# Local attention after a recurrence: V as the stationary operand, and the softmax divided ahead of the transposes

## The chip, the cores and the metric

The kernel runs on one core of a Trainium2 chip. The metric is the device time of one execution in microseconds: the median of three runs was 3732.54 us (3727.72 to 3736.64). The profile is that of one more execution, which took 3730.44 us.

In this document PE is TensorE (matrix products), PEld its loads of stationary operands, DVE is VectorE, ACT is ScalarE, POOL is GpSimd and SP is SyncE, which issues most of the transfers.

## The reference

The input x has 8 sequences of 512 tokens with 128 features. Everything is in float32.

1. x is normalised and goes through a recurrence over the 512 tokens, `h = tanh(h @ A.T + xb_t)`, `y = h @ C.T`; the result is normalised and added to x.
2. Then come six layers. Each has local attention with 16 heads of 64 features and windows of 32 tokens, followed by a feed-forward layer with a GELU gate. In both, half of the features are first shifted by one token.

The part of the attention that matters here is:

```python
q = l2norm(q) * qs ; k = l2norm(k) * ksc        # then rotary tables
sim = einsum('bhwie,bhwje->bhwij', bq, bk2) * 8.0   # 32 queries, 64 keys
sim = where(mask, -max, sim)
attn = softmax(sim, -1)
out = einsum('bhwij,bhwje->bhwie', attn, bv2)
x = out @ Wo + x
```

A window of 32 queries looks at its own 32 keys and at the 32 before them.

## The kernel before, in words

The work of the attention is cut into **groups**. In layers 1 to 5 a group is one sequence and eight heads (class `Group`); in layer 0 it is a stretch of 128 tokens of four sequences and eight heads (class `ChunkGroup`), so that the attention can start while the recurrence still runs. There are 96 groups, 16 to a layer. The eight heads are four pairs (`GP = 4`); `par` names the head of a pair.

A group takes four **slots** (`slot(n, t)`, t = 0 to 3), one for each 128 queries. In slot t of group n the program issues work of four groups:

- the attention of group n itself (`cur`): `scores` (q times k, 32 products of 64 rows by 32 columns, added to a mask that ScalarE has written into the same PSUM tile `sc`), `less_max` (the maximum and the difference), `exps`, and `mask` for the next slot;
- the end of the attention of the slot before (`last`): `turn` transposes the exponentials and copies them to `eT`, `average` multiplies them with V, `divide` divides;
- preparation of group n + 1 (`one`): `sums`, `solve`, `spread` and `finish` normalise q and k (ten Newton steps on VectorE, L450 to L456, and four scalings, L565), `values` makes V, `between` moves halves of it by transfers;
- preparation of group n + 2 (`two`): `unit_a` and `unit_b` project q and k. Their PSUM tiles rawa and rawb are read by ScalarE (L530, L542, L544), VectorE (L516) and, through `bs`, POOL (L548, L549).

In slot 1 the group before (`old`) is multiplied with Wo (`project`, four steps) and added to the residual (`add`).

In the kernel before, `average` takes the exponentials as the stationary operand and V as the moving one, for each head and window. V has a 65th column of ones (`VW = DH + 1`), so the same product gives the sum of the exponentials:

```python
av[blk * QB : (blk + 1) * QB, i, :VW],
self.eT[rows, i, blk * QB : (blk + 1) * QB],   # stationary: 64 rows, 32 queries
self.v[rows, BT * t + blk, i, :],              # moving: 65 columns
```

The result has queries on the partitions. `divide` takes the reciprocal of the 65th column and multiplies, for each `par`; `turn_back` transposes the result one slot later and ScalarE copies it to `aoT`, which `project` reads.

The program is written under a manual schedule: each engine runs its instructions in the order in which the Python code issues them. `mixed` is that order for the groups that run beside the recurrence (the first nine), `dense` for all later ones. The recurrence is driven by `rec.tick(us)`: after enough issued work it puts one more step (a product with A, L281, and a tanh, L289) into the queues; where the attention needs tokens that the recurrence has not reached, `alone` runs steps with filler products. A `Feed` puts the feed-forward layer of four sequences beside a group: shifting and centring in slots 0 and 1, the products of L890 to L923 in slot 2. This is so for eleven groups with four sequences and for one near the end with two.

PSUM tiles come from pools: "acc" has two buffers, taken in turn by `turn`, `turn_back` and the two tiles of `average` (and by the output of the feed-forward layer); "mm" has four (three while the recurrence runs), for projections, values, sums and spreads. `sc` is a single tile.

Of the kernel before, what the change touches and what calls it, by code (L numbers as in the profile page):

```python
# [15 lines left out]
P = 128  # L16
# [11 lines left out]
GP = 4  # L28
# [7 lines left out]
VW = DH + 1  # L36
# [12 lines left out]
def mk_seq_preln_kernel(  # L49
# [44 lines left out]
    for i in range(2):  # L94
        vb = const.tile([P, NBLK, GP, VW], F32, name=f"vbuf{i}")
        nc.gpsimd.memset(vb, 0.0)
        nc.gpsimd.memset(vb[:, :, :, DH:], 1.0)
        vbufs.append(vb)
# [53 lines left out]
    with tc.tile_pool(name="qk", bufs=2) as qkp, tc.tile_pool(  # L152
# [323 lines left out]
        class Group:  # L476
# [174 lines left out]

            def turn(self, t):
                nm = f"{self.nm}_{t}"
                tp = accp.tile([P, GP, P], F32, tag="acc", name=f"tp_{nm}")
                for i in range(GP):
                    nc.tensor.transpose(  # L656
                        tp[:, i, :], self.e[:, i].rearrange("p a k -> p (a k)"), ident
                    )
                rec.tick(0.5)
                self.eT = ep.tile([P, GP, P], F32, tag="eT", name=f"eT_{nm}")  # L660
                nc.scalar.copy(self.eT, tp)  # L661

            def average(self, t):
                self.avs = [
                    accp.tile(
                        [P, GP, P], F32, tag="acc", name=f"av_{self.nm}_{t}_{par}"
                    )
                    for par in range(2)
                ]
                for i in range(GP):  # L670
                    for blk in range(BT):
                        for par, av in enumerate(self.avs):
                            rows = slice(par * KB, (par + 1) * KB)
                            nc.tensor.matmul(  # L674
                                av[blk * QB : (blk + 1) * QB, i, :VW],
                                self.eT[rows, i, blk * QB : (blk + 1) * QB],
                                self.v[rows, BT * t + blk, i, :],
                                start=True,
                                stop=True,
                                skip_group_check=True,  # L680
                            )
                rec.tick(0.8)

            def divide(self, t):
                nm = f"{self.nm}_{t}"
                self.ao[t] = ep.tile(
                    [P, GP, 2, DH], F32, tag="ao", name=f"ao_{nm}", bufs=1
                )
                for par, av in enumerate(self.avs):
                    rc = small.tile([P, GP], F32, tag="rc", name=f"rc_{nm}_{par}")  # L690
                    nc.vector.reciprocal(rc, av[:, :, DH])  # L691
                    nc.vector.tensor_mul(  # L692
                        self.ao[t][:, :, par, :],
                        av[:, :, :DH],
                        rc.unsqueeze(2).to_broadcast([P, GP, DH]),
                    )

            def turn_back(self, t):
                if t == 0:
                    self.aoT = aop.tile([P, GP, S], F32, tag="ao", name=f"aoT_{self.nm}")  # L700
                at = accp.tile([P, GP, P], F32, tag="acc", name=f"at_{self.nm}_{t}")
                for i in range(GP):
                    nc.tensor.transpose(  # L703
                        at[:, i, :], self.ao[t][:, i].rearrange("p a d -> p (a d)"), ident
                    )
                rec.tick(0.5)
                nc.scalar.copy(self.aoT[:, :, t * P : (t + 1) * P], at)  # L707
# [262 lines left out]
        def mixed(n, t, cur, one, two, old, last, lt, back, bt):  # L970
# [10 lines left out]
            if old and t == 1:  # L981
                fill[3] = [lambda: old.project(wo)]
# [22 lines left out]
            if back:  # L1005
                back.turn_back(bt)
# [10 lines left out]
            if one and t == 1:  # L1017
                one.finish(1)
            if last:
                last.average(lt)  # L1020
# [4 lines left out]
            if last:  # L1025
                last.divide(lt)
# [24 lines left out]
        def dense(t, cur, one, two, old, last, lt, back, bt, feed):  # L1051

            def softmax():
                if cur:
                    cur.less_max(t)
                    cur.exps()
                    if t + 1 < NT:
                        cur.mask(t + 1)
                    elif one:
                        one.mask(0)  # L1060

            if last:
                last.turn(lt)
            if back:
                back.turn_back(bt)
            u = 2 * t - 4
            if two and t >= 2 and not (feed and t == 2):
                two.unit_a(u)
            if cur:
                cur.scores(t)  # L1070
            if t == 0:
                softmax()
                if one:
                    one.sums()
                    one.values(0)
                    one.inv.solve()
                if feed:
                    feed.centre(range(0, feed.nb // 2))
                elif one:
                    one.values(1)  # L1080
                    one.between(0)
                if feed:
                    feed.centre(range(feed.nb // 2, feed.nb))
                elif one:
                    one.values(2)
                if last:
                    if not cur:
                        fill(2)
                    last.average(lt)
                    last.divide(lt)  # L1090
                if one:
                    one.spread(range(4))
                    one.finish(0)
            if t == 1:
                softmax()
                if old and not cur:
                    fill(1)
                if old:
                    old.project(wo, (0, 1))
                if one:  # L1100
                    one.finish(1)
                if last:
                    last.average(lt)
                    last.divide(lt)
                if old:
                    old.project(wo, (2, 3))
                    old.add()
                if one:
                    one.finish(2)
                    one.finish(3)  # L1110
# [8 lines left out]
            if t >= 2:  # L1119
                if two and not (feed and t == 2):  # L1120
                    two.unit_b(u)
                softmax()
                if last:
                    if not two:
                        fill(1)
                    last.average(lt)
                    if feed and t == 2:
                        feed.scale()
                    last.divide(lt)
# [14 lines left out]
        def slot(n, t, feed=None):  # L1144
# [10 lines left out]
            back, bt = (cur, t - 2) if t > 1 else (old, NT - 2 + t)  # L1155
            if n < NREC:
                mixed(n, t, cur, one, two, old, last, lt, back, bt)
            else:
                dense(t, cur, one, two, old, last, lt, back, bt, feed)
# [141 lines left out]
def _layout(i):  # L1301
# [17 lines left out]
    w = np.concatenate([qk, v], 2)  # L1319
    b1 = col(i["L0_ffn_b1"])  # L1320
    for base in (0, DI):
# [11 lines left out]
        "w_o": np.asarray(i["L0_ffn_Wo"]),  # L1333
# [24 lines left out]
```

## Time and profile before

| what | value |
|---|---|
| median of three runs | 3732.54 us (3727.72 to 3736.64) |
| the profiled execution | 3730.44 us; its span, first to last instruction, 3728.5 us |
| mean granted TensorE clock | 0.979 |
| a plain group of layer 3, from scores to scores (2005.18 to 2034.17) | 28.99 us |
| 0 to 177 us: the recurrence alone | TensorE busy 150.8 us, VectorE 75.3 |
| 177 to 626 us: groups beside the recurrence | TensorE busy 385.9 us, VectorE 253.0 |
| 912.8 to 3646 us: layers 1 to 5 | TensorE busy 2665.0 us of 2733.2, VectorE 2011.6, ScalarE 1517.5 |

How to read it: busy time is the time in which an engine had an instruction in work. The chain of work goes back from the last instruction, at each step to what released it, so its pieces are the work that set the end. In a line of a group of instructions, the numbers after the count are the busy time in us, the mean of one in ns, the idle time of the engine ahead of them, and what ended that. A matmul in float32 is two instructions.

### The profile page before, as it was taken

The numbers are of one execution on the slowest core, as the hardware profiler recorded it, in microseconds if no ns is written. First come the engines' busy times: TensorE is split into PE (matmuls) and PEld (weight loads), VectorE is DVE, ScalarE is ACT, GpSimd is POOL, SyncE is SP. The second block draws the span as 40 slices with busy tenths as digits, with TensorE's granted clock in tenths as the row PEclk, the third lists the DMA queues.
The fourth block names the chain that finished last, engine by engine and source line by source line (L and its number), as shares of the span: only waits on it lengthen the run. The fifth ranks groups of instructions, "written<-read, shape, count | busy, mean of one in ns | idle before, by whom it ended". The sixth has DMA issues, their size and how long they took to land.

```text
span 3728.5 us, 158927 instructions
## 1 busy us (share of the span) xinstructions
PE 3540.4 (95%) x70178; PEld 2134.8 (57%) x70180; DVE 2587.2 (69%) x5211; ACT 1929.4 (52%) x3864; POOL 1826.7 (49%) x780
## 2 busy tenths in 40 slices
PE   8888987999999999999999999999999999999998
PEld 4566654555566555556566566565566565566564
DVE  3455565767677677677677677677677677677674
ACT  2344443545556455455466455466456455455452
POOL 1442332636466366366366366366366466466460
PEclk9888988999999999999999999999999999999999
DMA  3233433554355355345355345355355355355352
GB/s 129 52 90 84 101 76 84 124 122 103 87 115 116 73 117 129 80 110 119 71 117 133 80 106 123 68 115 138 74 117 116 69 126 126 74 115 118 70 117 70
DMA packets 355866, 378.20 MB, mean 101 GB/s; under 512 B 93550, under 2 KB 254572, under 8 KB 355052
## 3 DMA queue, kind: packets, MB, share of 16 engines
q1 hardware_dynamic: 354172, 365.78, 42.8%
q8 instruction: 554, 9.08, 1.0%
q10 hardware_dynamic: 1008, 2.27, 0.2%
q14 instruction: 132, 1.08, 0.1%
HBM read 34.56 MB, written 14.20 MB: 13 GB/s over the span
## 4 chain that ended last, share of the span: by engine, by line
PE 80%; DVE 11%; ACT 4%; issue 3%; SPq 1%; DMA 1%; DVEq 0%; ACTq 0%
PE yo L713 8%; PE rawb L538 8%; PE rawa L526 8%; PE sc L627 8%; PE av L674 5%; PE tp L656 5%; PE nsq L430 4%; PE at L703 4%; PE xb L281 3%; PE yf L916 3%; PE fa L890 3%; PE fg L894 3%; PE vps L587 3%; PE bc L465 3%; PE warm L361 2%
## 5 line engine op out<-in xcount | busy, mean ns | idle before, releaser
L548 POOL TENSOR_TENSOR u<-rope_sb,bs 128x1024 f32<-128x1024 f32 x320 | 766.4, 2395 | 1225.2 <-ACT bs L544 1090.0
L549 POOL TENSOR_TENSOR t<-t,u 128x1024 f32<-128x1024 f32 x320 | 756.8, 2365 | 25.1
L516 DVE SCALAR_TENSOR_TENSOR t<-rawa,par_sb,rope_sb 128x1024 f32<-128x1024 f32 x320 | 410.3, 1282 | 215.2 <-ACT sq L530 199.6
L650 ACT ACTIVATE e<-e 128x512 f32<-128x512 f32 x320 | 201.7, 630 | 371.4 <-DVE e L643 236.1
L565 DVE TENSOR_TENSOR t<-t,bc 128x1024 f32<-128x1024 f32 x320 | 381.7, 1213 | 15.0 <-PE bc L465 9.8
L661 ACT COPY eT<-tp 128x512 f32<-128x512 f32 x320 | 190.2, 594 | 353.0 <-PE tp L656 352.5
L674 PEld LDWEIGHTS av<-vbuf,eT 64*32 64x32 f32 x20480 | 227.3, 106 | 214.3 <-issue 138.1
L526 PE MATMUL rawa<-xbuf,wqk 128*128 128x512 f32 x640 | 342.8, 617 | 0.0
L538 PE MATMUL rawb<-xbuf,wqk 128*128 128x512 f32 x640 | 342.4, 617 | 0.0
L587 PE MATMUL vps<-wv,xbuf 128*64 128x256 f32 x2560 | 316.4, 387 | 8.4 <-DVE xf L864 8.4
L713 PE MATMUL yo<-aoT,wo 128*128 128x512 f32 x640 | 317.0, 618 | 0.3 <-ACT aoT L707 0.3
L627 PEld LDWEIGHTS sc<-kbuf,qT 64*32 64x32 f32 x20480 | 228.0, 105 | 144.7 <-ACT sq L542 57.6
L692 DVE TENSOR_TENSOR ao<-av,rc 128x256 f32<-128x256 f32 x640 | 271.5, 424 | 22.0
L674 PE MATMUL av<-vbuf,eT 64*32 64x65 f32 x20480 | 281.8, 225 | 3.7 <-issue 3.7
L627 PE MATMUL sc<-kbuf,qT 64*32 64x64 f32 x20480 | 282.8, 225 | 1.9 <-issue 1.8
L640 DVE TENSOR_REDUCE mx<-sc 128x8 f32<-128x512 f32 x320 | 219.3, 685 | 89.1 <-PE sc L627 89.0
L281 PEld LDWEIGHTS xb<-hT,s1w 128*128 128x128 f32 x1022 | 168.3, 197 | 173.8 <-ACT hT L289 118.7
L596 ACT COPY vbuf<-vps 128x512 f32<-128x512 f32 x320 | 188.1, 588 | 138.1 <-PE vps L587 134.7
L542 ACT ACTIVATE sq<-rawb 128x512 f32<-128x512 f32 x320 | 189.8, 593 | 129.7 <-PE rawb L538 129.1
L587 PEld LDWEIGHTS vps<-wv,xbuf 128*64 128x64 f32 x2560 | 168.4, 136 | 152.1 <-DVE rc L691 48.5
L289 ACT ACTIVATE hT<-xb 128x8 f32<-128x8 f32 x512 | 91.5, 179 | 293.8 <-PE xb L281 278.5
L908 DVE SCALAR_TENSOR_TENSOR pr<-fa,b,gl 128x512 f32<-128x512 f32 x144 | 106.8, 748 | 183.0 <-ACT gl L902 178.9
(282 smaller groups left out, 6392.1 us busy)
## 6 DMA issues: line engine op xcount, KB each, us to landing
qT<-t SPq DMA_DIRECT2D x640, 128.0 KB
kbuf<-t SPq DMA_DIRECT2D x640, 128.0 KB
vbuf<-vbuf SPq DMA_DIRECT2D x544, 130.0 KB
vbuf<-vbuf SPq DMA_DIRECT2D x160, 97.5 KB
wqk<-in_w_qkv SPq DMA_DIRECT2D x12, 512.0 KB
xbuf<-xT SPq DMA_DIRECT2D x48, 128.0 KB
xf<-xT SPq DMA_DIRECT2D x24, 256.0 KB
xf<-xT SPq DMA_DIRECT2D x24, 255.5 KB
```

The lines of the kernel that those rows point to most:

```text
L281: nc.tensor.matmul(self.xb[:, k, :], abc[:, 0, :], self.hT[:, (t - 1) % P, :], start=False, stop=True, skip_group_check=True,)
L516: nc.vector.scalar_tensor_tensor(t, self.twice(raw), scale, self.rope(isk, 1), ALU.mult, ALU.mult)
L526: nc.tensor.matmul(raw, self.wqk[:, c, 0], self.xs[:, WINDOW:], start=True, stop=True)
L538: nc.tensor.matmul(raw, self.wqk[:, c, 1], self.xs[:, WINDOW:], start=True, stop=True)
L548: nc.gpsimd.tensor_mul(self.wide(u), self.rope(isk, 0), self.twice(bs))
L549: nc.gpsimd.tensor_add(self.ts[c], self.ts[c], u)
L565: nc.vector.tensor_mul(t, t, self.bcs[c].unsqueeze(1).to_broadcast([P, 2, S]))
L587: nc.tensor.matmul(ps[par * KB : (par + 1) * KB, j], self.xs[:, k0 : k0 + KB], self.wv[:, par * GP * DH : (par + 1) * GP * DH], start=True ...
L627: nc.tensor.matmul(self.sc[blk * QB : (blk + 1) * QB, par, i, :], self.qT[rows, i, q0 : q0 + QB], kT[rows, i, :], start=False, stop=True, ...
L674: nc.tensor.matmul(av[blk * QB : (blk + 1) * QB, i, :VW], self.eT[rows, i, blk * QB : (blk + 1) * QB], self.v[rows, BT * t + blk, i, :], s ...
L692: nc.vector.tensor_mul(self.ao[t][:, :, par, :], av[:, :, :DH], rc.unsqueeze(2).to_broadcast([P, GP, DH]),)
L713: nc.tensor.matmul(self.yp, wo[:, self.g * GP + c, :], self.aoT[:, c, :], start=(c == 0), stop=(c == GP - 1),)
```

## The change

`average` now takes V as the stationary operand (64 keys by 64 features) and the transposed exponentials as the moving one (32 queries). The result has features on the partitions, two heads to a tile: pairs i and i + 1 give the lower and upper half. ScalarE copies it to `aoT` straight away, in two copies of 256 columns, so `turn_back` and its call are gone. V has no column of ones any more. `divide` now works on the exponentials of the slot itself: a sum over the keys, a reciprocal that is written to a tile of "acc", and a product into a new tile `p`, which `turn` transposes in the next slot. The rows of Wo are ordered for the new pairing ahead of the launch. The order in `mixed` and `dense` changes with it: `scores` comes ahead of `turn`, in slots 2 and 3 `unit_a` follows `turn`, the average comes before `unit_b`, and in slot 1 the four steps of `project` come together ahead of the average.

```diff
-VW = DH + 1
+VW = DH
...
-        nc.gpsimd.memset(vb[:, :, :, DH:], 1.0)
...
+            def divide(self, t):
+                nm = f"{self.nm}_{t}"
+                sm = small.tile([P, GP, 2], F32, tag="rc", name=f"sm_{nm}")
+                nc.vector.reduce_sum(sm, self.e, AX.X)
+                rcp = accp.tile([P, GP, P], F32, tag="acc", name=f"rc_{nm}")
+                rc = rcp[:, :, :2]
+                nc.vector.reciprocal(rc, sm)
+                self.p = ep.tile([P, GP, 2, KB], F32, tag="p", name=f"p_{nm}")
+                nc.vector.tensor_mul(
+                    self.p, self.e, rc.unsqueeze(3).to_broadcast([P, GP, 2, KB])
+                )
+
             def turn(self, t):
...
-                        tp[:, i, :], self.e[:, i].rearrange("p a k -> p (a k)"), ident
+                        tp[:, i, :], self.p[:, i].rearrange("p a k -> p (a k)"), ident
...
             def average(self, t):
...
+                order = [
+                    (j + half, blk)
+                    for j in range(0, GP, 2)
+                    for blk in range(BT)
+                    for half in range(2)
+                ]
+                for i, blk in order:
+                    half = slice(i % 2 * DH, (i % 2 + 1) * DH)
+                    cols = slice(blk * QB, (blk + 1) * QB)
+                    for par, av in enumerate(avs):
+                        rows = slice(par * KB, (par + 1) * KB)
+                        nc.tensor.matmul(
+                            av[half, i // 2, cols],
+                            self.v[rows, BT * t + blk, i, :],
+                            self.eT[rows, i, cols],
...
+                for par, av in enumerate(avs):
+                    nc.scalar.copy(
+                        self.aoT[:, 2 * par : 2 * par + 2, t * P : (t + 1) * P],
+                        av[:, :2],
+                    )
...
-            def divide(self, t):
-                nm = f"{self.nm}_{t}"
-                self.ao[t] = ep.tile(
-                    [P, GP, 2, DH], F32, tag="ao", name=f"ao_{nm}", bufs=1
-                )
-                for par, av in enumerate(self.avs):
-                    rc = small.tile([P, GP], F32, tag="rc", name=f"rc_{nm}_{par}")
-                    nc.vector.reciprocal(rc, av[:, :, DH])
-                    nc.vector.tensor_mul(
-                        self.ao[t][:, :, par, :],
-                        av[:, :, :DH],
-                        rc.unsqueeze(2).to_broadcast([P, GP, DH]),
-                    )
-
-            def turn_back(self, t):
-                if t == 0:
-                    self.aoT = aop.tile([P, GP, S], F32, tag="ao", name=f"aoT_{self.nm}")
-                at = accp.tile([P, GP, P], F32, tag="acc", name=f"at_{self.nm}_{t}")
-                for i in range(GP):
-                    nc.tensor.transpose(
-                        at[:, i, :], self.ao[t][:, i].rearrange("p a d -> p (a d)"), ident
-                    )
-                rec.tick(0.5)
-                nc.scalar.copy(self.aoT[:, :, t * P : (t + 1) * P], at)
...
-        def dense(t, cur, one, two, old, last, lt, back, bt, feed):
+        def dense(t, cur, one, two, old, last, lt, feed):
+            u = 2 * t - 4
+            plain = two and t >= 2 and not (feed and t == 2)
+            if cur:
+                cur.scores(t)
             if last:
                 last.turn(lt)
-            if back:
-                back.turn_back(bt)
...
+            if cur:
+                cur.less_max(t)
+            if plain:
                 two.unit_a(u)
             if cur:
-                cur.scores(t)
+                cur.exps()
+                if t + 1 < NT:
+                    cur.mask(t + 1)
...
             if t == 1:
...
                 if old:
-                    old.project(wo, (0, 1))
+                    old.project(wo)
                 if one:
                     one.finish(1)
                 if last:
                     last.average(lt)
-                    last.divide(lt)
+                if cur:
+                    cur.divide(t)
+                if one:
+                    one.finish(2)
                 if old:
-                    old.project(wo, (2, 3))
                     old.add()
                 if one:
-                    one.finish(2)
                     one.finish(3)
...
             if t >= 2:
-                if two and not (feed and t == 2):
-                    two.unit_b(u)
-                softmax()
                 if last:
...
                     last.average(lt)
-                    if feed and t == 2:
-                        feed.scale()
-                    last.divide(lt)
+                if plain:
+                    two.unit_b(u)
+                if feed and t == 2:
+                    feed.scale()
+                if cur:
+                    cur.divide(t)
```

## The prediction

> **What bounds the kernel now.** I read the page's engine shares first, then its chain of work that ended last.
>
> ```profile
> span 3728.5 us, 158927 instructions
> ...
> PE 3540.4 (95%) x70178; PEld 2134.8 (57%) x70180; DVE 2587.2 (69%) x5211; ACT 1929.4 (52%) x3864; POOL 1826.7 (49%) x780
> ...
> PE 80%; DVE 11%; ACT 4%; issue 3%; SPq 1%; DMA 1%; DVEq 0%; ACTq 0%
> ```
>
> TensorE is nearly always busy and carries the chain, but shares say nothing of one stage. So I took one plain group of layer 3 (four slots, no feed-forward beside it), 2005.2 to 2034.2 us, and read the chain through it; this is its start.
>
> ```profile
> 2005.25 0.79 PE sc L627 x53
> 2006.04 1.05 PE rawb L538 x2
> 2007.10 0.79 PE av L674 x53
> 2007.89 1.05 PE rawa L526 x2
> 2008.94 0.87 PE rawb L538 x2
> 2009.82 0.64 PE tp L656 x4
> 2010.46 0.44 PE at L703 x4
> 2010.89 0.86 PE rawa L526 x2
> 2011.76 0.79 PE sc L627 x53
> ```
>
> All 31 pieces of that chain are TensorE's, so a plain group is TensorE's own work. A projection costs 0.86 us, and 1.05 right after a tiled operation (sc, av): leaving the tiles costs 0.19. Next, busy time in the four slots of the group (score to score: slots 2, 3, 0, 1).
>
> ```profile
> core 0: us, PE busy (x) PEld busy (x) DVE busy (x) ACT busy (x) POOL busy (x), PEclk, DMA share, GB/s
> 2005.18:2011.68 6.50, 6.50 (x145) 3.48 (x144) 5.72 (x10) 4.33 (x8) 3.22 (x2) 1.00 0.63 139
> 2011.68:2018.27 6.59, 6.59 (x151) 3.71 (x150) 4.58 (x9) 5.03 (x11) 6.51 (x4) 1.00 0.20 45
> 2018.27:2026.96 8.69, 8.69 (x257) 6.94 (x256) 7.08 (x19) 5.03 (x10) 8.53 (x4) 1.00 0.54 121
> 2026.96:2034.17 7.21, 7.21 (x147) 3.96 (x146) 5.68 (x10) 3.00 (x6) 0.69 (x1) 1.00 0.80 183
> ```
>
> The reader is to see how little room the others have: VectorE 23.1 us of 29.0, ScalarE 17.4, most of it in slots 2, 3 and 0. The granted clock is 1.00. Last, the groups that the change touches.
>
> ```profile
> L692 DVE TENSOR_TENSOR ao<-av,rc 128x256 f32<-128x256 f32 x640 | 271.5, 424 | 22.0
> L674 PE MATMUL av<-vbuf,eT 64*32 64x65 f32 x20480 | 281.8, 225 | 3.7 <-issue 3.7
> L643 DVE TENSOR_TENSOR e<-sc,mx 128x512 f32<-128x512 f32 x320 | 221.1, 691 | 11.0
> L640 DVE TENSOR_REDUCE mx<-sc 128x8 f32<-128x512 f32 x320 | 219.3, 685 | 89.1 <-PE sc L627 89.0
> L707 ACT COPY aoT<-at 128x512 f32<-128x512 f32 x320 | 193.8, 605 | 3.0 <-PE at L703 2.8
> L703 PE MATMUL at<-ident,ao 128*128 128x128 f32 x1280 | 192.4, 273 | 2.2 <-DVE ao L692 2.2
> L691 DVE RECIPROCAL rc<-av 128x4 f32<-128x4 f32 x640 | 111.4, 174 | 44.5 <-PE av L674 34.1
> ```
>
> **The change part by part**, per slot (384 in all: 96 groups of four).
>
> TensorE loses the four transposes back: 0.44 on the chain. The average keeps 32 products in two passes, 64 loads and 64 matmuls, but on four tiles of 64x64 instead of eight of 64x32: 16 passes a tile instead of 8. Loads become 64 columns, moved operands 32. No row has this form. Loads took 106 ns at 32 columns and 136 at 64 (the values, L587): 0.94 ns a column, 60 ns for 64. A 512-column matmul starts 0.43 us after the one before: 0.84 ns a column, 27 for 32. In the transposes 128 columns load and 128 move every 0.11 us, so the load hides behind the previous move, and a pass costs the longer of the two. Now that is the load: 16 x 60 = 0.96, with 0.15 of start 1.1 us instead of 0.79. I take 1.1, as the transposes are the nearest row for loads as long as the moves. Lower end 0.79 (same instruction count at the same pace), upper end 1.55: load and move one after the other, 16 x 87 = 1.39, and the start. In slot 1 the projection is no longer cut by the average, which saves two leavings and adds one for the transposes: 0.3. Per group TensorE's work changes by -4 x 0.44 + 4 x 0.31 - 0.3 = -0.8 us (-2.1 at 0.79, +1.0 at 1.55).
>
> Two rules speak on the average. The Trainium skill (TensorEngine Tiling (Array Packing), Instruction Overhead) says that a free dimension of 1 takes as long as 60, so a small dimension should not be made smaller: moving 32 instead of 65 would gain nothing, a pass would keep its 0.1 us (0.79 over 8 passes of a tile), and 16 passes would give 1.6; the total would then be near rival B's 4035. The same skill's TensorE: Matmul & The Clock Gate ("Wait — 56ns, not 53.3ns?") says that matmuls never start less than about 25 ns apart: 64 x 25 = 1.6, before as after, which would take 4 x 0.31 off a group's bill. Here 64 start within 0.64 us (the 0.86 that one average's matmuls span, less the 0.22 of the last), 10 ns apart: the second rule does not hold in this trace; whether the first does, no row shows.
>
> VectorE loses two reciprocals and two products, 2 x (0.17 + 0.42) = 1.20, and gains a sum (0.685, as the maximum L640), a reciprocal (0.17) and a product over 512 (0.69, as L643): 1.55, so 1.4 more per group. The ends of the new rows are near: 0.6 and 0.7. ScalarE loses a copy of 512 columns (0.605) and gains two of 256. With 0.18 for 8 columns (L289) and 0.60 for 512, 256 cost 0.385: 0.77, 0.17 more; ends 0.30 and 0.60 each.
>
> The order is what costs. Before, the transposes took the exponentials themselves; division came after the average and fed only the transposes back, a slot later. Now sum, reciprocal and product stand between the exponentials and the transposes. The reciprocal goes to a tile of the pool "acc", which has two buffers, taken in turn by tp, av, av, rc. So the reciprocal waits until ScalarE has copied the first av, and that average stands late in TensorE's order. Behind the waiting reciprocal VectorE's queue holds the product, two of the scalings L565 (1.21 each), the residual addition and the next maximum.
>
> I laid the four slots out by hand, each engine in program order with the rows' durations, 0.20 us from a matmul's end to its reader and 0.04 to 0.05 between other engines. The old order comes to 28.96 us a group (measured 28.99). The new one, from the scores of slot 1:
> - TensorE: scores 0.0, transposes, four projection steps to 4.97, average 5.07 to 6.08, scores of slot 2 to 6.79.
> - VectorE: sum to 4.63, then idle for 2.1 us; ScalarE's first copy ends at 6.67, product 6.92 to 7.61. TensorE's transposes start at 7.66: wait 0.8.
> - VectorE is now late: scaling, addition, scaling to 10.56, the maximum of slot 2 10.50 to 11.19, difference 11.92, exponentials 12.60, mask 13.18. The scores of slot 3 wait 0.3.
> - Product of slot 2 14.03 to 14.72: transposes wait 0.75.
> - ScalarE, held behind these exponentials, still owes five readings of slot 2's projections (L542, L544, L530, L542, L544: 3.2 us) before it copies the transposes at 17.70: the average of slot 3 waits 1.5.
>
> Another 0.2 goes before the projection; then the values give the queues time to catch up. Layout against layout, TensorE's work with its changes of tiling goes from 28.4 to 27.4 (-1.0, near the -0.8 above) and its waits from 0.5 to 3.5; a group takes 30.9: **+1.9 us**. It is +1.2 with an average at 0.79, +2.9 at 1.43, +3.3 at 1.55 (a longer average eats some of the waits).
>
> 75 groups are plain: 75 x 1.9 = +143 us. Twelve have a feed-forward beside them: its products hide lateness in slot 2, but slot 1 is VectorE's (two scalings and a Newton solve behind the same reciprocal), ends +0.5 and +3, taken as +2: +24. In the nine first groups the recurrence fills in: each slot loses a transpose and the step after it (0.65 us, as these follow each other in the trace), some 33 slots, -21; the thirty steps that go, by the new program's order, are run alone later at 0.655, +20; longer averages +11, one wait fewer or more unknown (-10 to +20): about +5.
>
> POOL's products (18.95 us a group) start some 2.4 us later, since their input is read after the average; 10 us of idle time cover that, and the key transfers on SP's queue, issued behind the L565 scalings, follow 2 us later into 13 us of margin. SP issues the same transfers (130 KB become 128), and POOL two memsets fewer at the start. These cost nothing while a group stays over 21 us.
>
> Sum: 3730.4 (the profiled run's time, 2 us under the median) + 143 + 24 + 5 = 3902; **3900**. Own range of this case 3830 to 4000 (averages of 0.79 and 1.43, with feed-forward and recurrence at their ends).
>
> **Rivals.** (A) Faster: the product is ready when TensorE comes to transpose, and -0.8 x 87 groups makes 3665. For it: VectorE and ScalarE sum to 25 and 20 of 29 us. Against: their work is bunched in slots 1 to 3. It decides where TensorE's waits grow by less than 0.8 us a group. (B) Load and move do not overlap on a tile: 1.55, 75 x 3.3 + 36 + 20 = +304, 4035. For it: no row shows a long load behind a short move more than twice in a row (the recurrence's pairs, 128 columns loaded and 8 moved, span 0.39 us, so start 0.13 apart). Against: the transposes. (C) VectorE's operations overlap by more than 0.05 us, or the copies take 0.3: half the waits go, 75 x 0.5 + 12 = +50, 3780. (D) The waits just eat the gain: a group within 0.1 us of 29.0, 3730.
>
> **How the numbers follow.** Forecast 0.58; B 0.08; C 0.17; A 0.14; D 0.03. The range must leave out no more than 2 in 10: it drops A, D and half of B, so 3750 to 4020. About 0.2% is what a measurement of this kernel can tell from none: faster 0.14, same 0.03, slower 0.83 (forecast, B and C).
>
> **What would show it.** The average near 1.1 us; L657's reciprocal waiting for the aoT copy L703, about 2 us in slot 1; transposes waiting for VectorE's product, an average waiting for the eT copy; plain groups near 30.9 us and TensorE's share of the chain below 80%. Wrong if plain groups fall below 29.0, or if the average alone explains the rise.

## The result, and the profile after

The changed kernel takes 3787.06 us, the median of four runs (3785.48 to 3788.05); the kernel before, on the same chip, 3730.39 (four runs, 3727.72 to 3736.64; the 3732.54 further up is the median of three of them). The ratio is 1.0149 (95% interval 1.0132 to 1.0167): slower by 57 us, where 170 were forecast. Engine shares of the page, and the shares of its chain of work that ended last:

```profile
span 3785.4 us, 155759 instructions
...
PE 3451.3 (91%) x68702; PEld 2117.0 (56%) x68704; DVE 2714.3 (72%) x4827; ACT 1965.1 (52%) x4248; POOL 1825.7 (48%) x778
...
PE 61%; DVE 23%; ACT 12%; issue 3%; DMA 1%; SPq 0%; ACTq 0%; DVEq 0%
```

TensorE is busy 89 us less, and yet the span is 57 us longer. TensorE's share of the chain falls from 80% to 61%; VectorE and ScalarE take what it gives up. Busy time in the four slots of a plain group of layer 3 (score to score: slots 2, 3, 0, 1):

```profile
core 0: us, PE busy (x) PEld busy (x) DVE busy (x) ACT busy (x) POOL busy (x), PEclk, DMA share, GB/s
2003.64:2010.60 6.96, 6.16 (x149) 3.47 (x157) 6.40 (x9) 3.08 (x7) 0.00 (x0) 1.00 0.68 155
2010.60:2019.22 8.62, 7.39 (x157) 4.14 (x164) 7.19 (x11) 7.76 (x17) 6.96 (x3) 1.00 0.29 63
2019.22:2027.41 8.19, 8.19 (x261) 6.46 (x268) 6.44 (x17) 5.27 (x10) 8.03 (x5) 1.00 0.46 116
2027.41:2033.67 6.26, 6.18 (x148) 3.62 (x156) 4.44 (x6) 1.70 (x3) 3.96 (x2) 1.00 0.77 172
```

The second column against the first shows TensorE's idle time: 0.80 us in slot 2, 1.23 in slot 3, next to nothing in slots 0 and 1. In the group as a whole TensorE's work is 27.9 us of 30.0; before it was 29.0 of 29.0. The chain of work that ended last, through slots 2 and 3 of this group:

```profile
2003.73 0.38 ACT aoT L703
2004.13 0.22 DVE rc L657
2004.36 0.02 issue
2004.38 0.69 DVE p L659
2005.07 1.13 DVE t L564
2006.20 0.60 DVE xT L723
2006.80 1.13 DVE t L564
2007.92 0.61 DVE mx L639
2008.56 0.70 DVE e L642
2009.30 0.04 issue
2009.35 0.63 ACT e L649
2009.98 0.48 ACT sc L616
2010.46 0.57 ACT aoT L703 x2
2011.03 0.50 ACT sq L541
2011.53 0.58 ACT bs L543
2012.11 0.49 ACT sq L529
2012.59 0.30 ACT sq L541
2012.89 0.04 issue
2012.93 0.73 ACT bs L543
2013.66 0.48 ACT eT L672
```

For ten microseconds no piece is TensorE's. The chain begins where the first average has been copied (L703), passes the reciprocal that waited for that copy, VectorE's queue behind it, the exponentials, and ScalarE's queue down to the copy of the transposes, for which the average of slot 3 (2014.18) waits. The waits of this stretch stand in the timeline (start, duration, engine and line; in brackets the idle time before it, and what ended that):

```profile
2004.13 0.21 DVE L657 RECIPROCAL rc<-sm 128x8 f32<-128x8 f32 x1 [2.28 <-ACT aoT L703]
2005.21 0.63 PE L667 MATMUL tp<-ident,p 128*128 128x128 f32 x4 [0.80 <-DVE p L659]
2012.21 0.63 PE L667 MATMUL tp<-ident,p 128*128 128x128 f32 x4 [0.75 <-ACT bs L543]
2014.18 1.23 PE L693 MATMUL av<-eT,vbuf 64*64 64x32 f32 x64 [0.48 <-ACT eT L672]
```

The third wait is put down to L543, which ended 0.04 us after the product that these transposes read. Last, the new groups of instructions:

```profile
L693 PE MATMUL av<-eT,vbuf 64*64 64x32 f32 x20480 | 371.7, 221 | 38.5 <-ACT eT L672 37.0 <-DMA xf<-xT 1.0
L659 DVE TENSOR_TENSOR p<-e,rc 128x512 f32<-128x512 f32 x320 | 219.8, 687 | 11.4 <-DVE rc L657 0.3
L654 DVE TENSOR_REDUCE sm<-e 128x8 f32<-128x512 f32 x320 | 216.5, 677 | 8.6 <-ACT e L649 8.6
L667 PE MATMUL tp<-ident,p 128*128 128x128 f32 x1280 | 208.6, 285 | 112.3 <-DVE p L659 59.5 <-ACT bs L543 51.5 <-issue 1.1
L703 ACT COPY aoT<-av 128x256 f32<-128x256 f32 x640 | 205.9, 374 | 231.7 <-PE av L693 231.7
L657 DVE RECIPROCAL rc<-sm 128x8 f32<-128x8 f32 x320 | 67.4, 211 | 239.3 <-ACT aoT L703 213.3 <-issue 2.3 <-DVE sm L654 0.5
```

The reciprocal is 67 us of work with 239 us of idle time ahead of it, 213 of them until L703.

For all plain groups together I took the starts of the first score product of each slot from the traces. There are 74 plain groups whose end lies before the last group's start, eleven groups with a feed-forward layer of four sequences, and the nine first. The middle value of each slot over the 74 gives an undisturbed group; the mean includes disturbances.

| per plain group, us | slot 0 | slot 1 | slot 2 | slot 3 | sum | mean |
|---|---|---|---|---|---|---|
| before | 8.67 | 7.21 | 6.50 | 6.59 | 28.96 | 29.57 |
| after | 8.20 | 6.26 | 6.96 | 8.62 | 30.04 | 30.34 |

A slot runs from score to score, and the change moves the scores to the head of the slot, so a slot of one kernel does not hold quite the work of the same slot of the other; the sums can be compared.

The difference of the spans, 56.9 us, divides into +56.5 (plain groups), -12.1 (feed-forward groups, 770.2 to 758.1), +13.5 (up to the end of the nine first) and -1.0 (the last two groups and the end).

### The profile page after: what moved, and what is told of

Same layout as the page of the kernel before. It is cut to its first block, busy times and chain, and to the rows that moved or that the text cites. A ratio compares the mean times of both kernels' runs of the same rounds, so it can differ in the third digit from the quotient of the medians.

```text
span 3785.4 us, 155759 instructions
## 1 busy us (share of the span) xinstructions
PE 3451.3 (91%) x68702; PEld 2117.0 (56%) x68704; DVE 2714.3 (72%) x4827; ACT 1965.1 (52%) x4248; POOL 1825.7 (48%) x778
## 4 chain that ended last, share of the span: by engine, by line
PE 61%; DVE 23%; ACT 12%; issue 3%; DMA 1%; SPq 0%; ACTq 0%; DVEq 0%
PE yo L712 8%; DVE t L564 6%; PE av L693 6%; PE rawb L537 4%; PE vps L586 4%; PE nsq L429 4%; PE sc L626 4%; PE xb L280 3%; PE yf L915 3%; PE fa L889 3%; PE fg L893 3%; ACT bs L543 2%; PE rawa L525 2%; DVE p L659 2%; PE tp L667 2%
## 5 line engine op out<-in xcount | busy, mean ns | idle before, releaser
L547 POOL TENSOR_TENSOR u<-rope_sb,bs 128x1024 f32<-128x1024 f32 x320 | 767.0, 2397 | 1267.4 <-ACT bs L543 1267.4
L548 POOL TENSOR_TENSOR t<-t,u 128x1024 f32<-128x1024 f32 x320 | 757.7, 2368 | 25.1
L693 PEld LDWEIGHTS av<-eT,vbuf 64*64 64x64 f32 x20480 | 336.2, 135 | 253.9 <-ACT eT L672 157.5
L693 PE MATMUL av<-eT,vbuf 64*64 64x32 f32 x20480 | 371.7, 221 | 38.5 <-ACT eT L672 37.0
L564 DVE TENSOR_TENSOR t<-t,bc 128x1024 f32<-128x1024 f32 x320 | 387.5, 1211 | 0.1
L525 PE MATMUL rawa<-xbuf,wqk 128*128 128x512 f32 x640 | 327.2, 593 | 0.0
L703 ACT COPY aoT<-av 128x256 f32<-128x256 f32 x640 | 205.9, 374 | 231.7 <-PE av L693 231.7
L667 PE MATMUL tp<-ident,p 128*128 128x128 f32 x1280 | 208.6, 285 | 112.3 <-DVE p L659 59.5
L712 PE MATMUL yo<-aoT,wo 128*128 128x512 f32 x640 | 297.0, 607 | 6.1 <-DVE t L564 1.0
L657 DVE RECIPROCAL rc<-sm 128x8 f32<-128x8 f32 x320 | 67.4, 211 | 239.3 <-ACT aoT L703 213.3
L543 ACT ACTIVATE bs<-rawb,par_sb 128x512 f32<-128x512 f32 x320 | 224.9, 703 | 20.8 <-POOL u L547 20.4
```

What stands on the lines that cost most here:

```text
L525: nc.tensor.matmul(raw, self.wqk[:, c, 0], self.xs[:, WINDOW:], start=True, stop=True)
L543: nc.scalar.activation(bs, raw, AF.Copy, scale=par_sb[:, self.l, 2 * isk + 1 : 2 * isk + 2])
L547: nc.gpsimd.tensor_mul(self.wide(u), self.rope(isk, 0), self.twice(bs))
L548: nc.gpsimd.tensor_add(self.ts[c], self.ts[c], u)
L564: nc.vector.tensor_mul(t, t, self.bcs[c].unsqueeze(1).to_broadcast([P, 2, S]))
L667: nc.tensor.transpose(tp[:, i, :], self.p[:, i].rearrange("p a k -> p (a k)"), ident)
```

## The experiments

Two theories to begin with. **W**: the reciprocal's wait for a buffer of "acc", and the lateness that it hands on, costs the time. **L**: what costs is the work itself, VectorE's 1.4 us more a group (or the longer average). Line numbers in a profile are those of the kernel that was run. Ratios are to the kernel before on the same chip; for comparison, the change has 1.0149.

### No division at all (e2)

```diff
-                sm = small.tile([P, GP, 2], F32, tag="rc", name=f"sm_{nm}")
...
-                nc.vector.tensor_mul(
-                    self.p, self.e, rc.unsqueeze(3).to_broadcast([P, GP, 2, KB])
-                )
+                self.p = self.e
```

> The changed kernel without the division: the sum, the reciprocal and the product are left out, and the transposes take the exponentials themselves, so the output is not normalised. What is left is TensorE's side of the change: four transposes fewer and a longer average. Theory W: without the wait TensorE's own work, about 1 us a group less than before, sets the time: a plain group of 27.3 to 27.9, 3580 to 3630. Rival P (the longer average, 1.06 us instead of 0.79, and its tilings cost what the transposes saved): a plain group stays at 28.9 and the time at 3720 to 3740.

3604.28 us, ratio 0.9642 (0.9620 to 0.9664). An undisturbed plain group takes 27.56 us (8.20, 6.12, 6.11, 7.12). TensorE's side of the change is a gain, with the longer average in it: P falls. What the division adds is 183 us (3787 less 3604; by the ratios 189).

### Less work for VectorE, the same wait (e3)

```diff
+                self.mx = mx
...
-                sm = small.tile([P, GP, 2], F32, tag="rc", name=f"sm_{nm}")
-                nc.vector.reduce_sum(sm, self.e, AX.X)
+                sm = self.mx.rearrange("p a i -> p i a")
```

> The changed kernel without the sums: the reciprocal takes the row maximum in place of the sum, so the output is divided by the wrong number; VectorE's load falls by 0.68 us a slot, 2.7 us a group, but the reciprocal still waits for the copy of the first average. Theory W: the idle time before the reciprocal grows by what the sum took, and the time stays within 15 us of the changed kernel's 3787. Rival L: VectorE's load is what is paid, so 2.7 us less of it, twice the 1.4 that the change added, takes the group back below the 28.9 of the kernel before: 3690 to 3730.

3779.32 us, ratio 1.0120 (1.0103 to 1.0136); a group of 30.01 us, after 30.04. The waits by engine and line, whole run:

```profile
DVE rc L657 <- ACT aoT L703: 373.3, 308, 4.5
```

The numbers are us in total, times, and the longest. In the changed kernel this wait was 213.3 us. The 160 us more are three quarters of the 216 that the sums took: the reciprocal waits instead of VectorE working, and the time falls by 8 us only. L falls for the sums.

### The reciprocal in SBUF (e1)

```diff
-                rcp = accp.tile([P, GP, P], F32, tag="acc", name=f"rc_{nm}")
-                rc = rcp[:, :, :2]
+                rc = small.tile([P, GP, 2], F32, tag="rcp", name=f"rc_{nm}")
```

> The changed kernel with one edit: the reciprocal goes to a tile in SBUF instead of a tile of the two-buffer PSUM pool acc, so it no longer waits for ScalarE's copy of the first average. VectorE does the same work. Theory W (the wait of the reciprocal and the lateness that it passes on cost the time): the groups' wait of 2.1 us in slot 1 goes, TensorE's waits for the product fall to almost nothing, and a plain group falls from 30.0 us to about 27.7 to 28.2 (a layout by hand, ScalarE's independent operations started 0.11 us before the last one's end, gives 27.70 where it gives 29.78 for the change as it is): 74 x -2 = -150, feed-forward groups -10, so 3610 to 3650, faster than the kernel before. Rival L (the cost is VectorE's added load of 1.4 us a group, with the longer average): the load stays, 3760 to 3800.

3823.34 us, ratio 1.0238 (1.0218 to 1.0257): slower than the change, and outside both expectations. Groups of instructions:

```profile
L658 DVE TENSOR_TENSOR p<-e,rc 128x512 f32<-128x512 f32 x320 | 472.7, 1477 | 28.0 <-PE rawa L525 1.4
L656 DVE RECIPROCAL rc<-sm 128x8 f32<-128x8 f32 x320 | 65.0, 203 | 11.0
```

The wait is gone, 239 us of idle time became 11. But the product, the same instruction with its second operand in SBUF instead of PSUM, takes 1477 ns in the mean instead of 687. The timeline at the end of one slot 0 shows why:

```profile
1992.38 2.39 POOL L547 TENSOR_TENSOR u<-rope_sb,bs 128x1024 f32<-128x1024 f32 x1
1992.72 0.20 DVE L656 RECIPROCAL rc<-sm 128x8 f32<-128x8 f32 x1
1992.96 2.36 DVE L658 TENSOR_TENSOR p<-e,rc 128x512 f32<-128x512 f32 x1
1994.85 2.69 POOL L548 TENSOR_TENSOR t<-t,u 128x1024 f32<-128x1024 f32 x1
1995.47 0.30 PE L666 MATMUL tp<-ident,p 128*128 128x128 f32 x1 [1.27 <-DVE p L658]
```

The columns are start, duration, engine and line; a line of the transposes closes it. The product starts while POOL's L547 runs and ends 0.55 us after it, and the transposes wait. Of the 384 products of the run 188 start during an operation of POOL, and these end 0.548 us after the end of that operation (0.545 to 0.552 for nine in ten), after 1.0 to 2.82 us. The other 196 take 691 to 694 ns. In the changed kernel, with one operand in PSUM, 187 products start during an operation of POOL and take 686 to 690 ns. POOL's L548 rises from 2.37 to 2.53 us in the mean. The Trainium skill (SBUF — State Buffer, "SBUF: two separate sides") describes an exclusive lock on a port pair that VectorE, when both of its inputs are in SBUF, shares with a GpSimd operation that reads SBUF, as L547 and L548 do: whichever starts first has it for the whole instruction. These numbers agree.

So this run says two things. Slots 2 and 3 take 6.07 and 7.12 us, what they take without any division (6.11 and 7.12): there the wait was what cost. Slot 1 takes 7.9 us in some groups and 9.5 to 10.0 in others (middle value 9.56): the product of slot 0 is held by POOL, its transposes stand at the head of slot 1, and where VectorE's scaling L564 behind it comes latest, the projection is late too. The PSUM tile that the change uses for eight numbers a row keeps VectorE clear of POOL, and it is this tile that makes the reciprocal wait.

### The average two steps earlier (e4)

```diff
-                    old.project(wo)
+                    old.project(wo, (0, 1))
...
                     last.average(lt)
...
+                    old.project(wo, (2, 3))
```

> The changed kernel with the average of slot 1 two projection steps earlier: steps 0 and 1, average, steps 2 and 3, which is the order of the kernel before. The copy of the first average follows 1.7 us earlier, and with it the reciprocal; TensorE pays one more change of tiling, 0.2 us a group. Theory W: most of the reciprocal's wait in slot 1 goes, a plain group falls to about 28.1 to 28.6 (layout by hand 28.06 against 29.78): 74 x -1.6, 3650 to 3690. Rival L: nothing goes and the change of tiling is added, 3785 to 3805.

3801.22 us, ratio 1.0182 (1.0163 to 1.0200), L's number. But the run did not do what it was made for, as the waits by engine and line show:

```profile
DVE rc L657 <- ACT aoT L703: 225.0, 92, 3.3
ACT aoT L703 <- PE yo L712: 205.8, 79, 3.1
```

In one plain group (n = 45) the average starts at 3.48 us of slot 1 instead of 5.20, but its copy at 6.62 instead of 6.44: the copy now waits for the projection's last product (206 us in all, second line). `aoT` has one buffer, and the old one is read until the projection ends. The wait to be shortened stayed, and nothing is told about W. The 0.2 us a group are the one change of tiling more.

### The reciprocal in PSUM, in a place that is free (e5, e5b)

The tile `sc` covers two banks of PSUM of which the scores fill one half each.

```diff
-                rcp = accp.tile([P, GP, P], F32, tag="acc", name=f"rc_{nm}")
-                rc = rcp[:, :, :2]
+                if t == 1:
+                    rc = sct[:, 1, GP * KB : GP * KB + 2 * GP].rearrange(
+                        "p (i a) -> p i a", a=2
+                    )
+                else:
+                    rcp = accp.tile([P, GP, P], F32, tag="acc", name=f"rc_{nm}")
+                    rc = rcp[:, :, :2]
```

> The changed kernel with the reciprocal of slot 1 in the unused half of the PSUM bank that holds the scores; the other slots keep their acc tile. The reciprocal of slot 1 then waits only for the sum, and the product still reads one operand from PSUM, so it should keep 0.69 us, where the product with both operands in SBUF took 2.1 to 2.8 us whenever POOL worked beside it. Theory W (the wait and the lateness passed on): a plain group as without the division, 27.5 to 28.0 (27.56 there, layout by hand 27.7), feed-forward groups' slot 1 back from 10.6 to about 8.9, and a total of 3600 to 3650, faster than the kernel before. Rival L (VectorE's load, or the division's place in the chain itself): 3720 to 3790.

3632.11 us, ratio 0.9717 (0.9702 to 0.9732). All of VectorE's work is there, and the kernel beats the one before by 2.8%. The group falls to 27.86 us (8.20, 6.26, 6.07, 7.33), slot 1 of the feed-forward groups to 8.90. The engine shares of its page and the shares of its chain:

```profile
PE 3440.6 (95%) x68702; PEld 2116.5 (58%) x68704; DVE 2718.5 (75%) x4827; ACT 1979.1 (54%) x4248; POOL 1824.6 (50%) x778
...
PE 92%; DVE 2%; issue 2%; ACT 2%; SPq 1%; DMA 1%; ACTq 0%; DVEq 0%
```

VectorE's timeline in one slot 1 (start, duration, engine and line):

```profile
1945.02 0.68 DVE L654 TENSOR_REDUCE sm<-e 128x8 f32<-128x512 f32 x1
1945.81 0.21 DVE L662 RECIPROCAL sc<-sm 128x8 f32<-128x8 f32 x1
1946.12 0.69 DVE L664 TENSOR_TENSOR p<-e,sc 128x512 f32<-128x512 f32 x1
```

The reciprocal follows the sum at once, the product keeps 0.69 us, and VectorE's share of the chain falls from 23% to 2%. VectorE's busy time is the same as in the change to 0.2%. W holds: one instruction's wait, in one slot of four, with the lateness that it hands on, is worth 155 us (161 by the ratios).

The same place in all four slots (`rc = sct[...]` without the condition):

> The same with the reciprocals of all four slots in the scores' bank. There the scores of the next slot, which write that bank, have to wait for the product. Theory W: slots 0, 2 and 3 had no long wait for the acc tile, so nothing is gained over the run with slot 1 alone, and slot 0, whose product ends 0.4 us after the next scores could start, loses up to 0.6 us a group: 0 to +50 us on that run. Rival: the acc tile is scarce in every slot, and this run is faster than that one by over 10 us.

3698.44 us, ratio 0.9896 (0.9881 to 0.9911), 66 us over the run with slot 1 alone, more than the 50 that W allowed. In the undisturbed group slot 0 grows by 0.44 and slot 2 by 0.51, slots 1 and 3 fall by 0.38 and 0.21; the mean group is 0.62 longer. The direction was right, but slot 2 and the disturbances were not foreseen. The place is good only where its bank's next writer comes late enough.

### More readings for ScalarE (e6)

```diff
+                xx = tmp.tile([P, S], F32, tag="xx", name=f"xx_{nm}", bufs=1)
+                nc.scalar.copy(xx, raw)
```

> The changed kernel with one more ScalarE reading of 512 columns behind each bs (four a group, two of them ahead of the copy of the transposes in slot 3), its result unused. If ScalarE's queue sets the end of slots 3 and 0 and independent operations start 0.11 us before the last one ends (as 1545 pairs of the kernel before do in the mean), the layout gives +0.94 us a plain group, 3850 to 3865. If durations are added end to end, as in the prediction, +1.16 us or more: 3870 to 3885. If ScalarE's queue sets nothing: 3785 to 3795.

3893.32 us, ratio 1.0415 (1.0398 to 1.0431). More than all three numbers. The total is not what separates the sizes, though: the undisturbed group grows by 0.99 us (slot 3 from 8.62 to 9.60, the other slots unchanged). That is nearer the 0.94 of overlapping durations than the 1.16 of durations end to end. Of the other 34 us between the spans, 12 came in the nine first groups, some 17 in disturbed plain groups, 4 with the feed-forward layer and 1 at the end; nothing tells why. That ScalarE's queue sets the end of slot 3 is shown: two readings more, and the slot is 0.98 longer.

### Where the disturbances of the kernel before came from (e8, e9)

The mean plain group of the kernel before is 0.6 us above the undisturbed one, that of the change 0.3. The largest part sits in slot 0. The chain of the kernel before in one such group:

```profile
1317.11 1.88 PE nsq L430 x63
1318.99 1.39 issue
1320.38 0.28 PE nsq L430
```

63 of the 64 products of the norms are done, and then TensorE stands still for 1.4 us, with no releaser. Behind the nine first groups there are 17 stops in which such a product starts over 1 us after the one before, and none in the change. In the trace's records of transfers each stop ends 1.3 to 1.6 us after the end of a 16 KB transfer of kind "instruction" on one queue, which has 554 of them, one to some 253 of TensorE's 140,358 instructions, or one in 6.7 us. First I tried whether their place alone matters:

```diff
+        pad = accp.tile([P, GP, P], F32, tag="acc", name="pad")
+        for _ in range(16):
+            nc.tensor.transpose(pad[:, 0, :], ident, ident)
```

> The kernel before with 16 transposes of the identity more at the start, into a tile that nothing reads: 64 more TensorE instructions, 2 us at most, nothing else changed. In the kernel before, TensorE stops 17 times for over 1 us inside the norms' 64 products, with no releaser, each time 2.2 to 3.0 us after a 16 KB transfer of its instruction queue began. If the stops come from where those transfers fall, the shift by 64 of 256 instructions moves them: the number of stops over 1 us in those products changes by 8 or more and the time by 10 to 25 us either way. If they have another cause (ScalarE, DMA, the clock), the same stops stay and the time is within 3 us of the kernel before.

3734.52 us, ratio 0.9999 (0.9987 to 1.0012), with 20 stops. They moved (8 of the 17 groups are stopped in both), and each again ends 1.2 to 1.5 us after the end of such a transfer, but their number hardly changed. Neither expectation holds whole: the place moves the stops, and does not remove them. Then one part of the change alone, in the kernel before:

```diff
+            if cur and t == 0:
+                cur.scores(t)
             if last:
                 last.turn(lt)
...
-            if cur:
+            if cur and t > 0:
                 cur.scores(t)
```

> The kernel before with one part of the change alone: in slot 0 of the groups after the first nine the scores stand ahead of the transposes and the transposes back, as in the changed kernel, so that 12 or so slow TensorE instructions come between the scores and the norms' products instead of none. Theory F (the stops of over 1 us inside the norms' products, 17 in the kernel before and none in the changed one, come from instructions that arrive too late after the scores' and norms' long run of short instructions): the stops fall to 5 or fewer and the time by 12 to 25 us, to 3708 to 3722. Rival (they come from something else that the change alters, or from where the transfers happen to fall): 12 or more stops stay and the time is within 5 us of the kernel before.

3708.16 us, ratio 0.9929 (0.9912 to 0.9945), and no stop. The norms' products among the groups of instructions (busy time, mean ns, then the idle time ahead of them) of the kernel before:

```profile
L430 PE MATMUL nsq<-sq,sel_sb 128*32 128x128 f32 x5120 | 166.1, 274 | 19.8 <-issue 19.7
```

and of this one:

```profile
L430 PE MATMUL nsq<-sq,sel_sb 128*32 128x128 f32 x5120 | 157.1, 274 | 0.0
```

The undisturbed group is as before (28.94). So the order "scores, transposes, norms" in place of "transposes, scores, norms", which belongs to the change, is worth 0.7% by itself. That the stops are TensorE waiting for instructions fits all three runs; no run varied the transfers themselves. Nor does the order rule such stops out: of the changed kernel's variants here, e1, e2, e4 and e5 have one each and e5b two, of 1.05 to 3.4 us.

### The bill

If the parts add, which the sum allows, in per cent of the kernel before: scores ahead -0.7 (e9), the rest of TensorE's savings -2.9 (e2 less e9), the division's work +0.8 (e5 less e2), the wait of the reciprocal in slot 1 and its lateness +4.3 (the change less e5): +1.5.

## Why the prediction was right in sign and three times too high

**Right.** The mechanism: VectorE's reciprocal idle for 2.3 us in slot 1 until L703 (2.1 forecast), the transposes of slot 2 waiting 0.8 us for the product, slot 3 waiting for ScalarE. E5 shows it by taking it away. The average's length: 1.06 us from its start to that of the next products (1.1 taken; 0.79 and 1.55 were the ends), so a pass did not keep the 0.1 us which the prediction had worked out from the skill's rule, and which gave 1.6: 16 passes took some 0.06 us each. The rule itself is not refuted by that, as 60 columns at the 0.84 ns taken are 0.05 us. TensorE's work per group: 28.99 to 27.92, so -1.07, for -1.0 in the layout. Sum 0.677, product 0.687, reciprocal 0.211 (0.17 taken), copies 0.374 (0.385). Rival A had the right price and condition: with the product ready in time the kernel takes 3632 (3665 was said, though 0.8 us off 87 groups make 3661). Rival B fell with the average's length, D with the result.

**Wrong: the size of a plain group, +1.9 for a measured +1.1 undisturbed.** TensorE's waits came to 2.1 us a group where the layout had 3.5. One by one, in the order of the layout, and as the group shown above has them (the middle values of the 74 plain groups lie within 0.1 us of these):

| TensorE waits, us | layout | measured |
|---|---|---|
| before the projection | 0.2 | 0.08 |
| transposes of slot 2 | 0.8 | 0.80 |
| scores of slot 3 | 0.3 | 0 |
| transposes of slot 3 | 0.75 | 0.75 |
| average of slot 3 | 1.5 | 0.48 |

VectorE's part came out as laid out: in the group shown above, counted from the start of the scores of the slot 1 ahead of it (1997.30 us), the exponentials of slot 2 end at 12.68 (12.60 forecast) and the mask at 13.16 (13.18). From there ScalarE is faster than forecast: its copy of the transposes ends at 16.84 where the layout has 17.70, and the average of slot 3 waits 1.0 us less. So the step that failed is "ScalarE ... still owes five readings of slot 2's projections (... 3.2 us)": it adds durations end to end. In the chain above two copies and five readings, from 2010.46 to 2013.66, take 3.20 us; the durations of their rows (0.374 twice, 0.62, 0.617 twice, 0.703 twice) add up to 4.01. In the kernel before, 1545 pairs of ScalarE's operations already overlap, the second starting 109 ns before the first ends in the mean (durations are 613). The trace before the change shows this, and the prediction did not use it. With starts 0.11 us early the same layout, an estimate by hand, gives 28.65 for the old order and 29.78 for the new, +1.13. That the first layout met the old order (28.96 for 28.99) was luck: it had 28.4 us of TensorE's work and 0.5 of waits, where the trace has 28.99 and none. E6 shows the same step from the other side: two more readings ahead of the copy cost 0.99, or 0.49 each, where one lasts 0.61.

**Wrong: a price that was left out.** The layout was set against one quiet group (28.99), and its difference multiplied by 75. The mean group before was 29.57. The new order of scores and transposes removed the stops of TensorE, which I had costed at nothing: e9 puts it at 26 us. Undisturbed groups give 74 x 1.08 = 80 us, and fewer disturbances bring this to 56.5.

**Wrong: the feed-forward groups, +24 for -12.** The +2 lay between two ends and was not worked out. In one such group TensorE's busy time falls from 66.65 to 65.18 us and its idle time only grows from 3.2 to 3.6: in the mean of the eleven, slot 1 is 1.1 longer, as forecast in kind, but the other three together are 2.2 shorter. The wait in slot 1 was costed and the saving in the others was not.

**The nine first groups**, +5 with -10 to +20: +13.5. Without the division it is much the same (the tenth group starts at 674.0 us, after 672.9), so the division is not its cause; the cause stays open.

Rival C's number (3780) came nearest, but not for its reasons: the copies did not take 0.30, and it is ScalarE's overlap that was sized wrong in the terms tested here. Its other ground, that VectorE's operations overlap by more, made some 0.1 us here: ScalarE's first copy ends 0.14 late against the layout (6.81 for 6.67), and the maximum of slot 2, which VectorE reaches behind it, 0.04 (11.23 for 11.19).

## What to carry to other kernels

A small result in a pool of two buffers inherits every wait of that pool: ask who must free the buffer and where that instruction stands in its queue. Here the place of eight numbers a row was worth five times the arithmetic that made them. Before a layout by hand is trusted, measure how far operations of each engine start from each other, not how long they last, and set the layout against the mean of many groups, not against one quiet one; then ask what the new order does to the disturbances too.

## What the runs showed of the hardware that I had not expected

- A VectorE product with both operands in SBUF that starts during an operation of POOL ends 0.548 us after the end of that operation (188 products, up to 2.82 us instead of 0.69); with one operand in PSUM it takes 0.69 whatever POOL does.
- TensorE can stand still in the middle of a run of short products with no releaser, with 1.1 to 1.8 us from one start to the next; such a stop ends 1.3 to 1.6 us after the end of a 16 KB instruction transfer. A dozen slower instructions between two such runs removed all 17 (in variants of the changed kernel, which has them too, one or two were left).
- 32 products with 64x64 stationary and 32 moving columns, in two passes each on four tiles, take 1.06 us from start to the next operation; with 64x32 stationary and 65 moving columns on eight tiles they took 0.79.
